# Adjacency layers with residual norms: where the second pair's norm steps and adjacency masks stand

## The chip, the cores and the metric

The kernel runs on one NeuronCore of a Trainium2 chip. The time is device microseconds of one execution; before the change the median of nine is 1879.75 us. TensorE multiplies matrices, VectorE, ScalarE and GpSimd do elementwise work and sums, SyncE issues the transfers. In the profile they are PE (its weight loads PEld), DVE, ACT, POOL and SP.

## The reference

There are 64 graphs of 256 nodes with 512 features, all float32. Two layers follow one another, each with a residual and a layer norm:

```python
deg = sum(adj, -1)                               # layer 0
agg = einsum('bij,bjf->bif', adj, x) / max(deg, 1e-6)
x   = layernorm(x + relu(concat([x, agg]) @ W.T))
q, k = split(x @ Wqk); v = x @ Wv                # layer 1
agg = einsum('bij,bjd->bid', adj, k * mask)
w   = mask * einsum('bid,bid->bi', q, agg) / sqrt(512)
x   = layernorm(x + softmax(w, over nodes)[:, :, None] * v)
```

The kernel folds Wq and Wk into one weight product (agg of x1 with q then stands for the scores), and masks adj by columns in place of masking k.

## The kernel before, in words

**Pairs and stages.** Two graphs are handled together, so there are 32 pairs, in the loop over `j` (line 760). A turn of the loop does layer 0 of pair `j` and layer 1 of pair `j - 1`. The first two turns are written out by themselves, since the pipeline is still filling: in turn 1, the normed features of pair 0 (`x1`) are transposed by TensorE (`turn_here`, line 625; its matmuls have line 629), while later turns send them through a transfer.

**Products in seven parts.** Each matrix product is made with seven block products in place of eight (the names P1 to P7). They need sums and differences of blocks of both operands: of the features (`outer_sums`, `fourth_sums`, `inner_sums`, tiles `xT_s`, `xT_i`, `x1T_s`, `x1T_i`, on VectorE and GpSimd), of the adjacency (`adj_sums`, tile `sa`, on GpSimd) and of the weights (`weight_sums`, tiles `t_i`, `t`, `w`, once, on VectorE). P1, P2, P3 and P5 are split once more by `inner` (line 340) into steps `first_two`, `second`, `third`, `last_two`; between them ScalarE copies PSUM banks that the next step's matmuls read or add into. At the end of P1 and P5 VectorE adds a fifth product to both banks (line 373) and, for P1, ScalarE then copies them to `own` (line 663). `own` holds the layer's result, `y` the operand of the aggregation, `z` its second half. `gather` (line 405) multiplies by the adjacency; its steps a to g are called u1, g2, g5, u2, u3, g3, u4.

**Order of the work.** Each engine works off its instructions in the order in which the program emits them. The order of the matmuls is written out by hand in strings: `run("i k m", ...)` takes the next step of unit i, then of k, then of m. The norms, masks, softmax and weight sums are side work: chains of small steps in `queue` (line 137). After each matmul step `tick` (line 152) looks for a chain's next step and emits it if its engine's planned time (`free`, by a cost formula) is not more than `room` ahead of the matmul clock: 0.6 us for VectorE and ScalarE. A `room` of -9.0 for VectorE shuts the planner's door on VectorE: its side steps stay in the queue, and in one chain a ScalarE step behind a VectorE step waits too. `quiet` stops the planner altogether. `flush(name)` (line 161) emits all that is left of a chain at that spot.

**The places that the change touches.** Layer norm 0 of pair 0 is queued at the end of turn 0 (`norm0`, line 525, rank 1): for each graph, two times `scaled` and `residual`, then `mean`, two `square`, `factor` (Ln and Exp), `shifts`, two `scale`. The masks of adj are four ScalarE steps (`mask_adj`, line 319, rank 4). The rest of the weight sums for layer 1 (`w1`, rank 9) is queued as well. In turn 1 the program runs P1, P5 and P2 interleaved (line 786), and later, once layer 0 is nearly done, transposes graph 0 of pair 0 (line 858), flushes the masks, makes the adjacency sums and loads rows of adj for pair 2 (lines 859 to 861), runs one step of P4, transposes graph 1 and makes the inner sums of the transposed features on GpSimd (line 864).

Of the kernel before, what the change touches and what calls it, by code (L numbers as in the profile page):

```python
# [94 lines left out]
def resnorm_kernel(  # L95
# [38 lines left out]
    gp = InOrder(tc, nc.gpsimd, clock, lambda name, n: 0.0)  # L134
    room = {vec: 0.6, act: 0.6}
# [25 lines left out]
    def flush(*names):  # L161
        while True:
            c = next((c for c in chains if not names or c[1] in names), None)
            if not c:
                return
            step(c)

    def run(order, **units):
        for name in order.split():
            units[name].pop(0)()  # L170
# [139 lines left out]
    def adj_sums(j):  # L310
        a, s = adjs[j], pool.tile([P, 4, 2, P], F32, name="sa", bufs=2)
        a11, a21, a12, a22 = (a[:, :, t, h * P:(h + 1) * P] for t in range(2) for h in range(2))
        gp.tensor_add(s[:, 0], a21, a22)
        gp.tensor_sub(s[:, 1], s[:, 0], a11)
        gp.tensor_sub(s[:, 2], a11, a21)
        gp.tensor_sub(s[:, 3], a12, s[:, 1])
        return {"A11": a11, "A12": a12, "A22": a22, "S1": s[:, 0], "S2": s[:, 1], "S3": s[:, 2], "S4": s[:, 3]}
# [307 lines left out]
    def turn_here(X, x1, k, ps):  # L625

        for t in range(NT):
            for c in range(NF):
                tc.keep_in_program_order(nc.tensor.matmul(  # L629
                    ps[t][:, c * P:(c + 1) * P], x1[:, k, t, c * P:(c + 1) * P], ident, is_transpose=True,  # L630
                    start=(c == 0), stop=True, skip_group_check=True))
            act.copy(X.a[:, k, :, :, t].rearrange("p h e m -> p (h e) m"), ps[t].rearrange("p (c m) -> p c m", c=NF))
# [125 lines left out]
    early = []  # L758

    for j in range(NP):  # L760
        X = Xs.pop(j)
        if j == 2:
            steady.append(True)
        flush("finish")
        owns[j] = pool.tile([P, 2, NT, F], F32, name="own", bufs=3)
        if j > 0:
            load_adj(j)
            run_now(late_sums)
            late_sums.clear()
            sumsA[j] = adj_sums(j)  # L770

        u, y, o = pf, py, pu
        ys[j] = pool.tile([P, 2, NT, F], F32, name="y")
        a1, a2, a3, a4, a5, a6, a7 = layer0(j, o, u, y)
        i = inner("P1", X, W0, pw[0], u, a1)
        k = inner("P5", X, W0, pw[1], y, a5)
        m = inner("P2", X, W0, pw[0], o, a2)
        p, q = pairs(u, X, S2, W0["T2"], a6), pairs(u, X, S3, W0["T3"], a7)
        r, s = inner("P3", X, W0, pw[1], y, a3), pairs(u, X, A22, W0["T4"], a4)
        if j == 0:  # L780
            run("i k i k i k i k", i=i, k=k)
            flush("degrees")
            load_rows(1)
        elif j == 1:
            early.append(a1)
            run("k i k m k i k", i=early[0], k=k, m=m)
            fourth_sums(X, [1])
            run("m p p", m=m, p=p)
            fourth_sums(X, [0])
            run("p p m", m=m, p=p)  # L790
            load_x(1)
        else:
            run("i k", i=i, k=k)
            send_scores(j - 2)
            run("i l k", i=i, k=k, l=open1)
            flush("norm")
            fetch_scores(j - 2)
            places[0](range(16))
            run("i k i k", i=i, k=k)
        if j != 1:  # L800
            fourth_sums(X, [1])
        if j > 1:
            flush("mask")
            sumsM[j - 1] = adj_sums(j - 1)
            if j + 1 < NP:
                load_rows(j + 1)
            load_x(j)
        if j > 1:
            softmax(j - 2)
            shared[0] = 1.0  # L810
        if j != 1:
            run("m p p", m=m, p=p)
            fourth_sums(X, [0])
            run("m p p m", m=m, p=p)
        flush("w0a")
        run("q q q", q=q)
        flush("w0")
        run("r q r m", m=m, q=q, r=r)
        if j == 1:
            flush("norm")  # L820
        quiet[0] = j < 2
        room[vec] = -9.0 if j > 1 else 0.6
        run("r s r", r=r, s=s)
        if j > 0:
            Y = x1Ts.pop(j - 1)
        if j > 1:
            inner_sums(Y, gp, 0)
            queue(1, "sums", *outer_sums(Y, vec), (vec, lambda Y=Y: inner_sums(Y, gp, 1)))
        T_late = []
        T = sums_T(ys[j], T_late, 0 if j < 2 else 1)  # L830

        if j == 0:
            degrees(1)
        zs[j] = pool.tile([P, 2, NT, HF], F32, name="z")
        g = gather(sumsA.pop(j), T, zs[j], pw[1], y[1], y[0], owns[j], rdegs[j], T_late)

        def sums_next():
            if j == NP - 1:
                return
            inner_sums(Xs[j + 1], gp, 0)  # L840
            rest = outer_sums(Xs[j + 1], gp)
            run_now(rest[:1])
            inner_sums(Xs[j + 1], gp, 1)
            late_sums.extend(rest[1:])
        if j == 0:
            sums_next()
            held = [c for c in chains if c[1] == "w1"]
            chains[:] = [c for c in chains if c[1] != "w1"]
            early.append(inner("P1", Xs[1], W0, pw[0], u, lambda fifth: early[1](fifth)))
            run("s s a b s c d i e i g f", s=s, i=early[0], **g)  # L850
            quiet[0] = False
        else:
            u2, o2, y2 = o, pf, y
            b1, b2, b3, b4, b5, b6, b7, b8 = layer1(j - 1, ys[j][:, :, 0], o2, u2, y2)
            jj = inner("P1", Y, W1, pw[0], u2)
            k = inner("P2", Y, W1, y[0], o2, b2)
            if j == 1:
                turn_here(Y, owns[0], 0, pw)
                flush("mask")
                sumsM[0] = adj_sums(0)  # L860
                load_rows(2)
                run("s", s=s)
                turn_here(Y, owns[0], 1, pw)
                inner_sums(Y, gp, 0)
                sums_Y = (*outer_sums(Y, vec), (vec, lambda: inner_sums(Y, gp, 1)))
                run("s a b s d c", s=s, **g)
                quiet[0] = False
                flush("w1")
                run("e j g f", j=jj, **g)
                queue(1, "sums", *sums_Y)  # L870
                run("k j k j k j", j=jj, k=k)
                b1(None)
                run("k", k=k)
            else:
                run("s s j s a b", s=s, j=jj, k=k, **g)
                room[vec] = 0.6
                run("j", j=jj)
                if j < NP - 1:
                    degrees(j + 1)
                run("c d j k e j", s=s, j=jj, k=k, **g)  # L880
                quiet[0] = True
                run("k", k=k)
                quiet[0] = False
                b1(None)
                run("g f", **g)
        flush("softmax", "adds", "sums", "degrees")
        if j > 0:
            aggs[j - 1] = late.tile([P, 2 * N_SIDE], F32, name="agg").rearrange(
                "p (k t f) -> p k t f", k=2, t=NT)
            vs[j - 1] = [late.tile([P, NT, F], F32, name="v", bufs=2) for _ in range(2)]  # L890
            T = sums_T(owns[j - 1])
            g = gather(sumsM.pop(j - 1), T, aggs[j - 1], pw[0], o2[1], o2[0])
            h, q = pairs(u2, Y, S2, W1["T2"], b6), pairs(u2, Y, S3, W1["T3"], b7)
            n = inner("P5", Y, W1, pw[1], y2, b5)
            p, open1 = pairs(u2, Y, A22, W1["T4"], b4), inner("P3", Y, W1, pw[1], y2, b3)
            norm0(j)
            mask_adj(j)
            run("k h h" if j > 1 else "h h", k=k, h=h)
            if j == 1:
                degrees(2)  # L900
                flush("degrees")
            if j < NP - 1:
                load_xT(j + 1)
            run("n k h h" if j > 1 else "n h h", k=k, n=n, h=h)
            fourth_sums(Y)
            shared[0] = 1.25
            sums_next()
            run("a n b q d q n c q e q n p g f", n=n, q=q, p=p, **g)
            b8()
            run("p l p l p l", p=p, l=open1)  # L910
            py, pu = pu, py
        else:
            norm0(0)
            mask_adj(0)
            chains.extend(held)
# [113 lines left out]
```

## Time and profile before

| | us |
|---|---|
| median of nine executions | 1879.75 |
| lowest and highest | 1878.16, 1880.83 |
| the profiled execution | 1880.45 |
| its span in the profile | 1878.6 |
| TensorE busy in the span | 1858.0 (99%) |
| VectorE busy | 1511.8 (80%) |
| ScalarE busy | 1308.9 (70%) |
| GpSimd busy | 908.8 (48%) |

A steady turn of the loop takes some 57 us: the transposed-operand matmuls of one turn that begin at 95.51 in the trace come again at 152.56. The granted clock of TensorE is 1.00 in that stretch. Rows of a timeline give the start in us from the span's start, the length, the engine, the line (90 for all that the three elementwise engines do, since a helper records it; 175 for matmuls, 629 for transposes), the operation, and the tile written and read; in brackets stand the idle time ahead of it and what ended that. A matmul of float32 with 512 columns advances TensorE by 0.86 us, one with 256 columns by 0.43; the lengths in the rows overlap with the row behind.

### The profile page before, as it was taken

Reading aid. Unit: us, or ns where it says so; the run is one execution under the profiler, and the core shown is the slowest. Engines: PE = TensorE matmul, PEld = TensorE weight load, DVE = VectorE, ACT = ScalarE, POOL = GpSimd, SP = SyncE. Lnnn points to the kernel's source line nnn. Section 1 sums busy time; section 2 is a strip of 40 time slices with the busy share of each in tenths; the row PEclk is TensorE's granted clock in tenths of the full one; section 3 lists DMA queues with packets and bytes.
Section 4 is the critical chain, followed back from the end, with each engine's and each line's share of the span. In section 5 each row is a group of like instructions: output and inputs, shape, how many; then the busy total and the mean of one; then the engine's idle time right before and its main releaser. Section 6 shows DMA issues by size and latency. Waiting matters only on the chain.

```text
span 1878.6 us, 25017 instructions
## 1 busy us (share of the span) xinstructions
PE 1858.0 (99%) x7002; PEld 1312.9 (70%) x7002; DVE 1511.8 (80%) x3180; ACT 1308.9 (70%) x3274; POOL 908.8 (48%) x1255
## 2 busy tenths in 40 slices
PE   9999999999999999999999999999999999999997
PEld 5667767767777677677677677677776777776775
DVE  7787888777888778887778887788877788877887
ACT  3667776777776677767677766777676777767766
POOL 5455453555443555444554435554445544355532
PEclk9999999999999999999999999999999999999998
DMA  6133334343333333343433343333434233433321
GB/s 225 57 74 82 99 90 119 85 104 88 101 96 99 104 85 98 96 111 85 110 83 101 95 103 100 85 100 99 106 85 115 80 101 95 110 94 85 100 64 51
DMA packets 380714, 181.27 MB, mean 96 GB/s; under 512 B 263712, under 2 KB 345248, under 8 KB 380576
## 3 DMA queue, kind: packets, MB, share of 16 engines
q1 hardware_dynamic: 380576, 179.67, 35.5%
q8 instruction: 57, 0.93, 0.2%
q14 instruction: 81, 0.66, 0.1%
HBM read 114.10 MB, written 34.06 MB: 79 GB/s over the span
## 4 chain that ended last, share of the span: by engine, by line
PE 94%; POOL 2%; issue 2%; DVE 1%; ACT 1%; POOLq 0%; ACTq 0%; DVEq 0%
PE bank L175 94%; POOL xT_i L90 1%; POOL xT_s L90 1%; POOL sa L90 1%; ACT own L90 1%; DVE v L90 0%; DVE own L90 0%; DVE turn L90 0%; ACT bank L90 0%; ACT x1T L90 0%; DVE bank L90 0%; PE bank L629 0%; DVE st L90 0%; ACT adj L90 0%; PE bank L652 0%
## 5 line engine op out<-in xcount | busy, mean ns | idle before, releaser
L90 ACT COPY bank<-bank 128x256 f32<-128x256 f32 (+1 forms) x768 | 332.5, 435 | 235.0 <-PE bank L175 222.3
L90 DVE TENSOR_TENSOR y<-bank,y 128x512 f32<-128x512 f32 x256 | 170.4, 686 | 132.7 <-ACT y L90 132.1
L90 ACT ACTIVATE own<-own,shift,rstd 128x512 f32<-128x512 f32 x255 | 199.8, 808 | 0.9 <-DVE shift L90 0.9
L175 PE MATMUL bank<-tv,sa 128*128 128x256 f32 x768 | 192.5, 380 | 0.9 <-DVE tv L90 0.9
L90 POOL TENSOR_TENSOR x1T_s<-x1T,x1T_s 128x256 f32<-128x256 f32 x64 | 63.6, 1012 | 267.8 <-PE bank L175 267.8
L90 POOL TENSOR_TENSOR x1T_i<-x1T_s 128x128 f32<-128x128 f32 x128 | 101.1, 790 | 183.1 <-DVE x1T_s L90 183.1
L90 ACT ACTIVATE junk<-own,less 128x512 bf16<-128x512 f32 x254 | 183.7, 723 | 3.0 <-DVE less L90 2.0
L175 PEld LDWEIGHTS bank<-tv,sa 128*128 128x128 f32 x768 | 145.4, 190 | 49.6 <-issue 22.9
L90 ACT COPY y<-bank 128x512 f32<-128x512 f32 x192 | 108.8, 583 | 95.2 <-PE bank L175 93.7
L90 POOL TENSOR_TENSOR sa<-adj 128x256 f32<-128x256 f32 x128 | 93.7, 732 | 167.6 <-DMA adj<-adj_t 153.8
L175 PE MATMUL bank<-w,x1T_s 128*128 128x512 f32 (+1 forms) x384 | 168.3, 521 | 0.0
L90 POOL TENSOR_TENSOR x1T_i<-x1T 128x256 f32<-128x256 f32 x64 | 55.1, 861 | 224.3 <-DMA x1T<-turn 211.5
L175 PE MATMUL bank<-t,xT_s 128*128 128x512 f32 (+1 forms) x384 | 159.7, 525 | 3.9 <-POOL sa L90 2.3
L90 DVE TENSOR_TENSOR v<-bank,v 128x512 f32<-128x512 f32 x186 | 119.1, 681 | 49.1 <-PE bank L175 49.1
L175 PE MATMUL bank<-t,x1T_s 128*128 128x512 f32 (+1 forms) x384 | 158.2, 521 | 0.3 <-ACT y L90 0.3
L175 PE MATMUL bank<-w,xT_s 128*128 128x512 f32 (+1 forms) x384 | 153.1, 521 | 0.0
L175 PE MATMUL bank<-t_i,xT_i 128*128 128x256 f32 x512 | 152.7, 380 | 0.3 <-POOL sa L90 0.2
L175 PE MATMUL bank<-t_i,x1T_i 128*128 128x256 f32 x512 | 152.2, 379 | 0.1
L175 PEld LDWEIGHTS bank<-t_i,x1T_i 128*128 128x128 f32 x512 | 97.1, 190 | 67.1 <-issue 49.8
L90 ACT COPY own<-bank 128x512 f32<-128x512 f32 x128 | 71.8, 587 | 92.8 <-PE bank L175 49.3
L175 PEld LDWEIGHTS bank<-t_i,xT_i 128*128 128x128 f32 x512 | 94.5, 189 | 58.3 <-issue 45.5
L175 PE MATMUL bank<-t,x1T 128*128 128x512 f32 x256 | 130.6, 592 | 0.0
(159 smaller groups left out, 4564.3 us busy)
## 6 DMA issues: line engine op xcount, KB each, us to landing
x<-x SPq DMA_DIRECT2D x64, 512.0 KB, 5.6
xT<-x_t SPq DMA_DIRECT2D x62, 512.0 KB, 5.5
out<-own SPq DMA_DIRECT2D x62, 512.0 KB, 3.2
x1T<-turn SPq DMA_DIRECT2D x480, 64.0 KB, 2.3
adj<-adj_t SPq DMA_DIRECT2D x64, 256.0 KB, 3.8
turn<-adj SPq DMA_DIRECT2D x64, 256.0 KB, 3.0
row<-d SPq DMA_DIRECT2D x31, 256.0 KB, 4.7
wqk<-wqk_t SPq DMA_DIRECT2D x4, 512.0 KB, 5.8
```

The costliest lines, as they stand in the source:

```text
L90: return self.tc.keep_in_program_order(getattr(self.engine, name)(out, *args, **kwargs))
L175: tc.keep_in_program_order(nc.tensor.matmul(ps, a, b, start=start, stop=True, skip_group_check=True))
```

## The change

In the second turn (`j == 1`) two things are different. First, after P1's and P5's first steps `room` of VectorE is set to -9.0 for the next five steps, and back to 0.6 behind them. In these steps the planner emits no VectorE side work; what is emitted directly, such as the additions at the end of P1 and P5, is not affected. Second, the flush of the masks, the adjacency sums and the load of rows stand behind the transposes of both graphs and the inner sums of the transposed features, where they stood between the two transposes. The order in which GpSimd makes `sa` and `x1T_i` is swapped by it. Since the planner's decisions depend on what was emitted before, the order of other side steps on VectorE and ScalarE in that turn differs too.

```diff
         elif j == 1:
             early.append(a1)
-            run("k i k m k i k", i=early[0], k=k, m=m)
+            run("k i k", i=early[0], k=k)
+            room[vec] = -9.0
+            run("m k i k", i=early[0], k=k, m=m)
+            room[vec] = 0.6
             fourth_sums(X, [1])
             run("m p p", m=m, p=p)
...
             if j == 1:
                 turn_here(Y, owns[0], 0, pw)
+                run("s", s=s)
+                turn_here(Y, owns[0], 1, pw)
                 flush("mask")
+                inner_sums(Y, gp, 0)
                 sumsM[0] = adj_sums(0)
                 load_rows(2)
-                run("s", s=s)
-                turn_here(Y, owns[0], 1, pw)
-                inner_sums(Y, gp, 0)
                 sums_Y = (*outer_sums(Y, vec), (vec, lambda: inner_sums(Y, gp, 1)))
                 run("s a b s d c", s=s, **g)
                 quiet[0] = False
```

## The prediction

> **What bounds the kernel now.** I read the page first, then the chain that ended last, then the list of who TensorE waited for, and last the timeline around the one pair that the change touches.
>
> ```profile
> span 1878.6 us, 25017 instructions
> PE 1858.0 (99%) x7002; PEld 1312.9 (70%) x7002; DVE 1511.8 (80%) x3180; ACT 1308.9 (70%) x3274; POOL 908.8 (48%) x1255
> ...
> PE bank L175 <- ACT own L90: 1.5, 4, 0.8
> ...
> PE bank L175 <- ACT x1T L90: 0.8, 1, 0.8
> PE bank L175 <- ACT y L90: 0.3, 1, 0.3
> PE bank L175 <- ACT bank L90: 0.3, 1, 0.3
> ```
>
> TensorE is busy 99% of the span and holds 94% of the chain, so an edit elsewhere counts only by the idle time it makes or removes on TensorE. The last lines give such waits over the whole span (total us, times, longest). The second pair runs once, from about 52 to 113 us of the span; before it hands over, TensorE waits there 0.82 us at 59.13, 0.35 at 69.71, 0.78 at 76.78 and 0.35 at 91.11. Removing all four would give 2.3 us, 0.12%: no gain of over 0.2% is there to be had. New waits have no such ceiling. TensorE's rows (start, length, operation, in brackets the idle time ahead and its releaser):
>
> ```profile
> 57.71 0.59 PE L175 MATMUL bank<-t_i,xT_i 128*128 128x256 f32 x2
> 59.13 3.67 PE L175 MATMUL bank<-t,xT_s 128*128 128x512 f32 x8 [0.82 <-ACT own L90]
> ...
> 69.71 0.67 PE L175 MATMUL bank<-w,xT_i 128*128 128x256 f32 x2 [0.35 <-ACT bank L90]
> 70.22 0.59 PE L175 MATMUL bank<-w,xT_s 128*128 128x256 f32 x2
> 70.65 1.02 PE L175 MATMUL bank<-t,agg 128*128 128x512 f32 x2
> 71.51 0.59 PE L175 MATMUL bank<-t_i,xT_s 128*128 128x256 f32 x2
> ...
> 76.78 1.99 PE L175 MATMUL bank<-y,adj 128*128 128x256 f32 x8 [0.78 <-ACT x1T L90]
> ```
>
> The same stretch on ScalarE and VectorE:
>
> ```profile
> 69.50 0.81 ACT L90 ACTIVATE own<-own,shift,rstd 128x512 f32<-128x512 f32 x1
> 70.42 0.57 ACT L90 COPY bank<-bank 128x512 f32<-128x512 f32 x1
> ...
> 73.97 1.31 ACT L90 ACTIVATE adj<-adj,mask_sb 128x256 f32<-128x256 f32 x3
> 75.18 0.58 ACT L90 COPY own<-bank 128x512 f32<-128x512 f32 x1
> 75.64 1.09 ACT L90 COPY x1T<-bank 128x512 f32<-128x512 f32 x2
> ...
> 57.93 1.42 DVE L90 TENSOR_TENSOR bank<-bank,fifth 128x256 f32<-128x256 f32 x4
> ...
> 60.56 0.68 DVE L90 TENSOR_TENSOR t<-t 128x256 f32<-128x256 f32 x1
> ...
> 66.71 0.42 DVE L90 TENSOR_TENSOR t_i<-w 128x256 f32<-128x256 f32 x1
> ...
> 83.22 0.69 DVE L90 TENSOR_TENSOR z<-bank,z 128x512 f32<-128x512 f32 x1
> ```
>
> **The change part by part.** No instruction is added or removed and TensorE's order is the same. What differs is the order on VectorE and ScalarE between 55 and 86 us and one swap on GpSimd; I compared the built orders of both kernels and priced the new order with the rows above, instruction by instruction.
>
> *Step 1, P1's additions first: a gain of about 1.0.* Before, VectorE ran four more norm steps of pair 0 (55.67 to 57.93), so the additions of the fifth product came at 57.93 though the products that they wait for (56.41 + 0.59) ended at 57.00; then ScalarE copied own from 58.40, and the matmul of 59.13 waited for it. Now the additions start at about 57.05, the first ends at 57.41, the copy runs 57.50 to 58.08, and the matmul starts at 58.23 (0.15 from the copy's end, as before: 58.40 + 0.58 to 59.13). That is 0.90 earlier. Up to 69.71 TensorE stays about 0.95 ahead: at that place ScalarE has the second square of the second batch element (0.72 a step) ahead of the bank copy, which I work out to 68.20 to 68.57, so the matmul comes at 68.72, 0.99 earlier, still with a wait of some 0.5.
>
> *Step 2, the norm steps arrive later: a new wait of 2.4.* The held steps of the second element (mean, two squares, Ln and Exp, the shift, two scalings) do not vanish. In the new order VectorE's shift stands behind the two 1024-wide weight sums, one y addition and the three additions to own (P2's end); and ScalarE has both scalings, which need that shift, ahead of the bank copy that P3's last matmuls read. That copy stood behind the scalings before too, but they were done by 70.31. VectorE: y addition 65.06 to 65.66 (starts: rows advance 0.60 to 0.64), weight sums 1.14 each to 67.94, y addition to 68.55, own additions 1.28 to 69.87, the one with the fifth to 70.48, shift done at 70.63. ScalarE: scalings from 70.70, 0.71 each to 72.12, bank copy 0.57 to 72.69. TensorE is through with the matmul ahead at 70.44 (68.72 + 0.43 + 0.43 + 0.86) and goes on at 72.84 instead of 71.51. So the lead of 0.99 turns into a lag of 1.33 (1.0 to 1.7 if each of the four hand-offs is 0.1 off). Queued behind that copy on ScalarE are the other copies of this stage, which wait for TensorE anyway.
>
> *Step 3, masks of adj: a gain of about 0.9.* Because VectorE is closed, the planner itself issues the three masks early on ScalarE (three of 0.40 at about 61.1 to 62.8, in slots where it waited for matmuls), so the flush behind the copies finds none left. The 1.31 of masks no longer stands between the transposes and the x1T copies. TensorE reaches the gather at 72.84 + 4.32 = 77.16, and the last x1T copy ends at 77.18 (own copy from 75.64, the x1T copies from 76.10, 0.51 apart, 0.57 long): start 77.23 against 76.78. The wait of 0.78 is gone; lag 0.45.
>
> *Step 4, VectorE's backlog of weight differences: a new wait of about 2.2.* Eight differences of w1 (P2's and P3's inner sums, 128x256) of which six were made at 66.71 to 70.0 now stand behind the last sum tv and ahead of the addition to z, which before started at 83.22. The matmul of 84.21 adds into the bank that this addition reads. New: tv's last sum starts at 81.69, the differences at 82.82 (before, 82.37). At the undisturbed pace (66.71 to 68.18: 1.47 for four) eight take 2.94, z runs 85.76 to 86.44, TensorE at 86.5. Beside GpSimd, whose eight sums now run 77.2 to about 84 (its rows: 2.9 and 3.7 a group of four), one of these took up to 0.68. If all eight took 0.68 (5.44), TensorE would go on at 89.0. I take 0.4 more than undisturbed, since GpSimd's work covers only the first two or three: 86.9, against 84.21 before: lag 2.7. Ends: 2.3 and 4.8.
>
> *Step 5, what moves at no cost.* GpSimd makes x1T's inner sums ahead of adj's: the first come earlier than they did relative to TensorE, and the adj sums are read from 98.52 on, over 10 us after they are made. x's load waits for the last residual addition of pair 0 on SP's queue (58.05 before, about 62 now), and the rows of adj and the next xT queue behind it; they take 3.0 to 5.6 us, and their first readers are at 94.02 (the degrees) and 100.06 on GpSimd, so 25 us are spare. If that cover were gone, 4 us would be lost. Past 87 us VectorE has slack of 1.85 at 90.0 and TensorE is full, so the lag stays to the end.
>
> The sum is -0.99 + 2.32 - 0.88 + 2.25 = 2.7 us. The profiled run took 1880.45 (span 1878.6, 1.85 around it), 0.70 above the median of 1879.75; its own time would become 1883.15, the median 1882.45. That is 0.14%.
>
> The granted clock is 1.00 in every stretch of this trace that I read, over waits of at most 0.9 us in them; a wait of 2.4 is not in it. [...]
>
> **The rivals.**
> - *VectorE's backlog decides (slower).* Over 0.2%, here 3.76 us and about what a measurement of this kernel can tell from no change, is reached when the eight differences of step 4 take 4.0 us, 0.50 each, rather than 3.34. For it: the 0.68 beside GpSimd, and tv rows of 1.12 and 1.21 against 0.68. Against it: GpSimd is done by about 84. At 0.55 each: +4.1, 1883.9; at the end of the rows +4.8.
> - *The clock or a further wait adds to the lags.* The longest wait of TensorE rises from 0.9 to 2.4; a disturbance that costs as much again as half of it is +3.9, 1883.7. Nothing in the trace shows one.
> - *The new waits do not come (gain).* If step 2's copy were ready when TensorE needs it and the backlog fitted the slots, only the removals remain: 0.99 + 0.78 = 1.8, 1878.0. Against it: the built order has both scalings ahead of that copy and all eight differences ahead of z.
> - *The change does nothing.* The masks' move alone would be the 0.78; but the order on both engines does change, so no.
>
> **How the numbers follow.** Forecast 0.63 (+1.6 to +3.6); backlog +4.1 0.16; clock or further wait +3.9 0.10; gain 0.09; nothing 0.02. Slower by over 0.2%: 0.26. Faster by over 0.2% would need more than every wait of the pair: 0.02. Within: 0.72. The range reaches from step 4's wait all but missing (2.7 - 2.1 = +0.6) to the end of the backlog case (+5.0): 1880.4 to 1884.8.
>
> **What would show it.** Right: matmul bank<-t,xT_s near 58.2; the first own scalings of the second element near 70.7 and a TensorE wait of about 2.4 <-ACT bank at 72.8; no wait <-ACT x1T of 0.78; eight t_i/w rows on VectorE at 83 to 86 and a wait of about 2.2 <-DVE z near 86.9. Wrong: a granted clock under 1.00 there, a first wait that stays at 59.1, or a lag that is worked off after 95 us.

## The result and the profile after

The changed kernel takes 1884.23 us (median of ten, 1882.06 to 1885.86) where the kernel before, with the runs made beside it, takes 1878.90 (median of thirty). The ratio is 1.0028, with a 95% interval of 1.0020 to 1.0036: the change costs 0.28%, between 3.8 and 6.8 us. The profiled execution of the changed kernel took 1883.76, with a span of 1882.0.

TensorE's waits over the whole span, the first two of the list, longest total first (total us, times, longest):

```profile
PE bank L175 <- ACT bank L90: 2.3, 2, 2.0
PE bank L175 <- DVE z L90: 2.2, 1, 2.2
```

The wait of 2.2 for z is new, and so is that of 2.0 in the first line (the other 0.3 of it was there before). Before, no wait of the second pair was over 0.82, and the longest in the whole span was 1.2, at the start. The wait of 0.78 for x1T and that of 0.82 for own are gone. TensorE's rows of the second pair in the changed kernel (start, length, operation, idle time ahead and its releaser):

```profile
57.98 3.67 PE L175 MATMUL bank<-t,xT_s 128*128 128x512 f32 x8
...
68.56 0.67 PE L175 MATMUL bank<-w,xT_i 128*128 128x256 f32 x2 [0.35 <-ACT bank L90]
...
72.52 0.79 PE L175 MATMUL bank<-t_i,xT_s 128*128 128x256 f32 x2 [2.00 <-ACT bank L90]
73.09 1.06 PE L175 MATMUL bank<-w,xT_i 128*128 128x256 f32 x2
73.95 1.91 PE L629 MATMUL bank<-ident,own 128*128 128x128 f32 x8
...
78.71 1.99 PE L175 MATMUL bank<-y,adj 128*128 128x256 f32 x8
...
88.87 1.13 PE L175 MATMUL bank<-y,sa 128*128 128x256 f32 x4 [2.19 <-DVE z L90]
89.84 0.83 PE L175 MATMUL bank<-t_i,x1T_i 128*128 128x256 f32 x2
90.45 1.06 PE L175 MATMUL bank<-w,x1T 128*128 128x256 f32 x2
91.31 1.92 PE L175 MATMUL bank<-t_i,x1T_i 128*128 128x256 f32 x4
```

The rows directly behind the two waits are to be looked at. Eight transposes of 1.04 us before (72.37) take 1.91 here, and four matmuls of t_i that took 1.35 before (85.93) take 1.92. The same engine does the same work more slowly. The table of stretches says why (columns: stretch, its length, then busy time of PE, PEld, DVE, ACT, POOL with instructions, then the granted clock, DMA share and GB/s):

```profile
70.50:72.50 2.00, 0.02 (x1) 0.00 (x0) 0.00 (x0) 2.00 (x4) 0.00 (x0) 1.00 0.24 75
72.50:75.90 3.40, 3.38 (x13) 3.01 (x14) 1.60 (x3) 0.85 (x3) 0.00 (x0) 0.57 0.00 0
75.90:79.30 3.40, 3.40 (x15) 1.84 (x15) 1.07 (x2) 2.15 (x4) 0.98 (x2) 0.92 0.00 0
79.30:86.70 7.40, 7.17 (x29) 4.83 (x27) 6.72 (x12) 2.11 (x4) 5.96 (x7) 1.00 0.00 0
86.70:88.90 2.20, 0.03 (x1) 0.03 (x1) 2.17 (x7) 0.00 (x0) 0.00 (x0) 1.00 0.00 0
88.90:92.30 3.40, 3.40 (x11) 2.64 (x12) 2.93 (x6) 0.36 (x1) 0.89 (x1) 0.67 0.00 0
92.30:95.70 3.40, 3.40 (x15) 2.68 (x14) 0.61 (x1) 2.44 (x6) 1.67 (x4) 0.83 0.00 0
```

In the first and fifth stretch TensorE stands still; in the two stretches behind each, the granted clock is 0.57 and 0.92, and 0.67 and 0.83. Lost at that clock are 3.4 x (0.43 + 0.08) = 1.7 and 3.4 x (0.33 + 0.17) = 1.7 us. In the profile of before the granted clock is 1.00 all the way from 4.7 to 1868 us.

The two engines that make the waits, in the changed kernel:

```profile
69.67 0.69 DVE L90 TENSOR_TENSOR own<-own,fifth 128x512 f32<-128x512 f32 x1
70.28 0.15 DVE L90 TENSOR_TENSOR shift<-less,rstd 128x2 f32<-128x2 f32 x1
...
83.55 1.21 DVE L90 TENSOR_TENSOR tv<-y,tv 128x512 f32<-128x512 f32 x1
84.68 0.94 DVE L90 TENSOR_TENSOR t_i<-w 128x256 f32<-128x256 f32 x1
...
87.80 0.42 DVE L90 TENSOR_TENSOR t_i<-w,t_i 128x256 f32<-128x256 f32 x1
88.13 0.68 DVE L90 TENSOR_TENSOR z<-bank,z 128x512 f32<-128x512 f32 x1
...
70.47 1.52 ACT L90 ACTIVATE own<-own,shift,rstd 128x512 f32<-128x512 f32 x2 [1.60 <-DVE shift L90]
71.89 0.57 ACT L90 COPY bank<-bank 128x512 f32<-128x512 f32 x1
```

ScalarE stands 1.60 us for the shift, which VectorE makes only behind the last addition to own; then come two scalings, and behind them the bank copy that TensorE waits for. Later VectorE goes through all eight weight differences (84.68 to 88.1) before the addition to z.

**Where the time went, in one account.** The changed execution is 0.33 us ahead before the change begins (its matmul of the pair's first step starts at 51.33, that of before at 51.66), so 0.33 is added to each difference. Lag behind before: -0.82 at the matmul of 57.98 (59.13 before), -0.82 at 68.56 (69.71), +1.34 at 72.52 (71.51), +2.26 at 78.71 (76.78), +4.99 at 88.87 (84.21), +6.45 at the adjacency matmul of 101.63 (95.51). From there to the end the two spans come 2.7 us closer, step by step at short waits of the later pairs: the execution of before has ten there for sa and three for own with 3.0 us in all, that of after six and one with 1.6, and each costs somewhat more than its length. These waits differ from profile to profile (three to eleven for sa in the kernels below), and the medians, 5.3 us apart, are the better measure.

### The profile page after: what moved, and what is told of

Same layout as the page of the kernel before. It is cut to its first block, busy times and chain, and to the rows that moved or that the text cites. A ratio compares the mean times of both kernels' runs of the same rounds, so it can differ in the third digit from the quotient of the medians.

```text
span 1882.0 us, 25016 instructions
## 1 busy us (share of the span) xinstructions
PE 1860.0 (99%) x7002; PEld 1315.5 (70%) x7002; DVE 1509.2 (80%) x3180; ACT 1309.5 (70%) x3274; POOL 910.7 (48%) x1255
## 4 chain that ended last, share of the span: by engine, by line
PE 94%; POOL 2%; DVE 2%; issue 1%; ACT 1%; POOLq 0%; DVEq 0%; ACTq 0%
PE bank L175 94%; POOL xT_i L90 1%; POOL xT_s L90 1%; POOL sa L90 0%; ACT own L90 0%; DVE own L90 0%; PE bank L629 0%; DVE v L90 0%; DVE tv L90 0%; DVE t_i L90 0%; ACT bank L90 0%; DVE turn L90 0%; DVE w L90 0%; DVE bank L90 0%; DVE st L90 0%
```

## The experiments

Two theories, A and B, stand against each other on what makes the loss, and a third, C, is on the clock: A (the held norm and weight steps make two waits, and each wait lowers the clock) and B (the second part of the change does, by the swap on GpSimd and the later loads), C (the low clock is not a consequence of the waits).

**One part alone: VectorE's closed door.**

```diff
-            run("k i k m k i k", i=early[0], k=k, m=m)
+            run("k i k", i=early[0], k=k)
+            room[vec] = -9.0
+            run("m k i k", i=early[0], k=k, m=m)
+            room[vec] = 0.6
```

> Only the first part of the change: VectorE takes no norm steps ahead of P1's last additions; masks, adjacency sums and the load of rows stay where they were. VectorE and ScalarE then run in the same order as in the whole change, since the planner issues the masks early by itself. Theory A (the loss of the whole change is two new waits of TensorE, each followed by some 1.5 to 1.9 us at a lower granted clock, both made by the norm and weight steps that were held back): still slower than before by 4.5 to 6 us, with both waits there; the second may be up to 0.4 shorter, since GpSimd makes the adjacency sums earlier. Theory B (the swap on GpSimd and the later transfers make the loss): within 1 us of before or faster by 0.8.

Measured: 1885.13 against 1878.97, ratio 1.0031 (1.0019 to 1.0043). This part alone is 6.2 slower, a little more than the 4.5 to 6 expected, and so makes all of the loss; B falls. The waits are not the same, though. TensorE's in the second pair of this kernel, and rows of VectorE and GpSimd:

```profile
PE bank L175 <- ACT bank L90: 3.8, 2, 2.9
PE bank L175 <- DVE z L90: 0.8, 1, 0.8
...
65.00 0.94 DVE L90 TENSOR_TENSOR t<-t 128x256 f32<-128x256 f32 x1
65.87 0.95 DVE L90 TENSOR_TENSOR t_i<-t,t_i 128x256 f32<-128x256 f32 x1
...
64.76 0.91 POOL L90 TENSOR_TENSOR sa<-adj 128x256 f32<-128x256 f32 x1
65.62 0.90 POOL L90 TENSOR_TENSOR sa<-adj,sa 128x256 f32<-128x256 f32 x1
```

The masks are early here too, so GpSimd makes the adjacency sums at 63 to 66.5, beside the weight differences on VectorE: these take 0.94 where they take 0.42 in the whole change. The shift comes at 72.12 in place of 70.28 (with the start 0.30 later, 1.5 of it is this), and the first wait grows to 2.9. In exchange GpSimd is free at 84.3, all eight later differences run at 0.42, and the wait for z is 0.78. Of the second part's two effects, the one is a gain and the other a loss of about the same size, which I had put at 0.4 and on one side only. Behind the wait of 0.78 the clock stays at 1.00; around and behind that of 2.9 it is 0.71 in 72 to 76 and 0.50 in 76 to 80.

**The other part alone: masks behind the copies.**

```diff
                 turn_here(Y, owns[0], 0, pw)
-                flush("mask")
-                sumsM[0] = adj_sums(0)
-                load_rows(2)
                 run("s", s=s)
                 turn_here(Y, owns[0], 1, pw)
+                flush("mask")
                 inner_sums(Y, gp, 0)
+                sumsM[0] = adj_sums(0)
+                load_rows(2)
```

> Only the second part: masks, adjacency sums and the load of rows behind the transposes. VectorE's and TensorE's orders are those of before; on ScalarE the three masks stand behind the x1T copies. Theory A: the wait of 0.78 for x1T goes, no new one comes, 0.8 us faster than before (too little to tell by time, plain in the trace). Theory B: slower than before by 2 us or more.

Measured: 1878.68 against 1878.97, ratio 0.9998 (0.9989 to 1.0007). The gather starts at 75.92 in place of 76.78, so the wait for x1T is gone, 0.86 gained. At 83.83 (84.21 before) 0.38 of it is left and at 95.23 (95.51) 0.28: a wait of 0.19 for tv is new, and GpSimd, whose sums now come later, runs beside VectorE's tv sums and a weight difference (0.94). A gain of 0.3 us, too little for the time to tell.

**The first wait alone taken away.** The norm's steps up to the shift stay where they were; its two scalings go behind P3's bank copies on ScalarE.

```diff
         if j == 1:
-            flush("norm")
+            for c in [c for c in chains if c[1] == "norm"]:
+                while len(c[3]) > NT:
+                    step(c)
...
         run("r s r", r=r, s=s)
+        if j == 1:
+            flush("norm")
```

> The whole change, but the two last scalings of the held norm stand behind the two bank copies of P3's third step on ScalarE; VectorE's order is that of the change. Theory A: the wait of 2.0 at 72.5 goes and with it the stretch of lower clock behind it (the gather starts near 74.8 in place of 78.7), the wait of 2.2 for z and the second low stretch stay: 3.9 us faster than the change, 1.4 to 2.5 slower than before. Theory C (the lower clock is not a consequence of the waits, or costs nothing): 2.0 faster than the change, about 3.3 slower than before, and the clock still under 1.00 in 72 to 80.

Measured: 1880.17 against 1878.97, ratio 1.0009 (1.0001 to 1.0018): 1.2 slower than before where 1.4 to 2.5 were expected, so some 4 us of the change's 5.3 are given back by moving two instructions of 0.8 behind two of 0.6 and 0.4. The gather starts at 75.91 in an execution that is 0.81 behind at the start of the pair, so at 75.10 when counted from before's start; the changed kernel's is at 79.04 by that count, 3.9 later. That is more than the wait of 2.0, as A says and C does not. But A's second half did not come out in this profile:

```profile
86.07 1.13 PE L175 MATMUL bank<-y,sa 128*128 128x256 f32 x4 [2.20 <-DVE z L90]
...
83.80:86.07 2.27, 0.07 (x2) 0.00 (x1) 2.24 (x7) 0.00 (x0) 0.00 (x0) 1.00 0.00 0
86.07:89.50 3.43, 3.37 (x14) 2.58 (x15) 2.96 (x6) 0.92 (x3) 0.89 (x1) 1.00 0.00 0
89.50:93.00 3.50, 3.23 (x15) 2.49 (x14) 1.38 (x3) 2.43 (x7) 1.68 (x4) 1.00 0.00 0
```

The wait of 2.20 is there, and the clock stays at 1.00. The eleven executions of this kernel lie in two groups, seven from 1879.09 to 1880.25 and four from 1881.60 to 1881.96, with the middle ones 2.0 apart; the profiled one is of the lower group. The mean granted clock of an execution, over its whole span, is 0.997 in all four of the upper group and 0.998 in six of the seven of the lower. The same wait thus seems to lower the clock in some executions and not in others.

**The second wait alone taken away.** All eight weight differences go behind both additions to z; the planner's clock for VectorE is kept as it was, so that nothing later moves.

```diff
-                flush("w1")
+                rest = next(c for c in chains if c[1] == "w1")
+                chains.remove(rest)
+                vec.free = max(vec.free, clock[0]) + len(rest[3]) * (0.07 + HF / 960)
                 run("e j g f", j=jj, **g)
+                planned = vec.free
+                run_now(rest[3])
+                vec.free = planned
```

> The whole change, but the eight weight differences that stood ahead of the addition to z stand behind both additions to z; ScalarE's order is that of the change. Theory A: the wait of 2.2 for z goes and with it the lower clock at 90 to 95: 3.7 us faster than the change, 1.6 to 2.8 slower than before; the wait of 2.0 at 72.5 and its low stretch stay. Theory C: 2.2 faster than the change, 3.1 slower than before.

Measured: 1882.98 against 1878.97, ratio 1.0021 (1.0012 to 1.0030), 4.0 slower than before where I had expected 1.6 to 2.8. The wait for z is gone, the clock stays at 1.00 behind 80 us, but there is a wait that I had missed (waits of the second pair):

```profile
PE bank L175 <- ACT bank L90: 2.3, 2, 2.0
PE bank L175 <- DVE t_i L90: 1.1, 1, 1.1
```

P2's first matmul of layer 1 reads the first two of those differences and comes right behind the addition to z. The wait of 2.0 stayed, with the clock at 0.69 in 72 to 76.

**Both waits taken away.** The edit of the third experiment, and of the eight differences the first two stay ahead of z.

```diff
-                flush("w1")
+                rest = next(c for c in chains if c[1] == "w1")
+                chains.remove(rest)
+                vec.free = max(vec.free, clock[0]) + len(rest[3]) * (0.07 + HF / 960)
+                planned = vec.free
+                run_now([rest[3].popleft() for _ in range(2)])
+                vec.free = planned
                 run("e j g f", j=jj, **g)
+                planned = vec.free
+                run_now(rest[3])
+                vec.free = planned
```

> The whole change with both new waits taken away: the two last scalings stand behind P3's bank copies on ScalarE, and of the eight weight differences only the two that P2's first matmul needs stay ahead of the addition to z, the other six go behind both additions. Theory A: no wait over 0.4 between 52 and 95 us, the granted clock 1.00 throughout, and of the step gains what the profile of the change showed stays: 0.8 at P1's copy and 0.8 at the x1T copies, less what later waits take back; the adjacency matmuls at the head of the stage come 1.0 to 1.8 earlier than before, measured from the same start, 0.05% to 0.1% faster and so hardly to be told by time. Theory C (the loss lies elsewhere in the change): still 2 us or more slower than before.

Measured: 1878.03 against 1878.51, ratio 0.9996 (0.9987 to 1.0006). All of the loss is gone. TensorE's longest waits in the second pair:

```profile
PE bank L175 <- ACT y L90: 0.5, 1, 0.5
PE bank L175 <- ACT bank L90: 0.3, 1, 0.3
```

The clock is 1.00 in every stretch from 52 to 115 us. The adjacency matmul starts at 94.84 (95.51 before, with this execution 0.10 behind at the start), so 0.8 is gained, a little under the 1.0 to 1.8 expected: a wait of 0.54 for y stands where one of 0.35 was, and a wait of 0.18 for tv remains. It is no version that the time can tell from before.

**What a wait costs by itself.** The kernel before, with dummy subtractions on VectorE ahead of an addition to z in 28 steady turns; a second kernel with fewer of them.

```diff
...
             act.copy(r22, of(u))
+            for _ in range(delay[0] if own is not None else 0):
+                tc.keep_in_program_order(nc.vector.tensor_sub(idle, idle, idle))
             vec.tensor_add(r22, of(p5), r22)
...
+        delay[0] = 8 + (j - 3) % 7 if 2 < j < NP - 1 else 0
```

> The kernel before, with dummy subtractions on VectorE (128x256, about 0.34 each) ahead of the first addition of the aggregation's u3 step in 28 steady turns, 8 to 14 of them, so that TensorE gets one wait of about 1.3 to 3.4 us in each turn, four of every length. It leaves no part of the computation out. [...] Theory A2 (a length decides): there is one length from which every wait lowers the clock and below which none does.

> The kernel before with the same dummy subtractions, but 4 to 7 of them in a turn: by the last run's step of 0.45 us for each more of them, waits of TensorE of about 0.4, 0.85, 1.3 and 1.75 us, seven of each. In the run with 8 to 14, waits of 2.2 to 2.8 lowered the granted clock in 7 of 8 turns, at 1.7 to 1.8 us each. [...] Theory A2 (one length near 2.0 to 2.2 decides): none in all 28 turns.

The first kernel took 2046.48 us and the second 1917.28, one execution each. The waits came out longer in the first than I had meant, 2.2 to 5.1. For every wait I took its length from TensorE's row, the granted clock of the 9 us behind it, and the time from its end to the adjacency matmul, 6.99 where the clock stays at 1.00:

| wait, us | turns | with a lower clock | time lost behind it |
|---|---|---|---|
| 0.36 to 0.53 | 7 | 0 | 0 |
| 0.82 to 0.83 | 7 | 0 | 0 |
| 1.28 to 1.40 | 7 | 0 | 0 |
| 1.74 to 1.86 | 7 | 0 | 0 |
| 2.20 to 2.77 | 8 | 7 | 1.6 to 1.7 |
| 3.12 to 3.71 | 8 | 7 | 1.4 to 3.0 |
| 4.04 to 5.08 | 12 | 12 | 2.4 to 3.0 |

C falls: waits put in by hand, with nothing else changed in TensorE's order, lower the clock. A2 falls too: of three waits of 2.20 and 2.21 in the first kernel two lowered it and one didn't, and a wait of 3.71 didn't. A wait of 2.20, one of 2.21 and that of 3.71 in the first kernel, each with the stretches behind it (columns as above):

```profile
202.90:206.20 3.30, 1.10 (x6) 0.62 (x5) 3.13 (x8) 1.33 (x5) 0.05 (x1) 1.00 0.00 0
206.20:209.60 3.40, 3.40 (x12) 2.37 (x13) 3.33 (x9) 3.10 (x6) 0.00 (x0) 1.00 0.00 0
209.60:213.00 3.40, 3.40 (x13) 2.28 (x12) 3.37 (x8) 2.88 (x9) 0.00 (x0) 1.00 0.63 184
...
1087.80:1091.10 3.30, 1.11 (x6) 0.62 (x4) 3.13 (x8) 1.37 (x5) 0.07 (x1) 1.00 0.02 5
1091.10:1094.50 3.40, 3.39 (x9) 2.56 (x10) 3.33 (x9) 3.07 (x6) 0.00 (x0) 0.64 0.00 0
1094.50:1097.90 3.40, 3.40 (x12) 2.08 (x11) 2.49 (x6) 1.26 (x4) 0.00 (x0) 0.86 0.66 177
...
1717.20:1722.00 4.80, 1.09 (x7) 0.61 (x5) 4.52 (x11) 1.35 (x5) 0.17 (x1) 1.00 0.00 0
1722.00:1725.40 3.40, 3.40 (x12) 2.38 (x13) 3.33 (x9) 3.09 (x6) 0.00 (x0) 1.00 0.00 0
1725.40:1728.80 3.40, 3.40 (x13) 2.28 (x12) 3.37 (x8) 2.89 (x9) 0.00 (x0) 1.00 0.69 189
```

Behind the second wait the clock is 0.64 and 0.86, behind the first and the third 1.00. So the length alone does not decide; what else does is left open. What a longer wait costs is also in the clock: over the 9 us behind a wait it is 0.81 to 0.84 where 1.4 to 1.7 us were lost, and 0.66 to 0.73 where 2.4 to 3.0 were.

By the two groups of times in the third experiment, with their middle ones 2.0 apart, one kernel seems to lose some 1.7 us at a wait in one execution and nothing in the next. The spread of the changed kernel fits this too: an estimate from the account above is 3.0 slower with neither wait hit (6.45 less twice 1.7) and 6.4 with both, against 1878.90 that is 1881.9 to 1885.3, and its executions took 1882.06 to 1885.86, with a mean granted clock of 0.998 and 0.997 in the two shortest (1882.06 and 1882.13) and 0.996 in the three longest (1885.43 to 1885.86). It was not seen in two profiles of one kernel.

## Why the prediction was right or wrong, point by point

- **The bound.** Right that no gain of over 0.2% was to be had. "Counts only by the idle time it makes or removes on TensorE" was too narrow: at the low clock TensorE lost some 3.4 us while it was busy.
- **Step 1, P1's additions first.** Right: 0.82 gained at the first matmul, 0.90 predicted; 0.82 at the second wait, where 0.99 was predicted.
- **Step 2, the norm steps arrive late.** Right in place and releaser, and near in size: a wait of 2.00 <-ACT bank where 2.4 was predicted, in part since TensorE came to it with a smaller lead (0.82, not 0.99); +1.34 of lag at that matmul against +1.33 predicted, and the shift at 70.28 and the scalings at 70.47, both within 0.35 of the working. The third experiment shows that the two scalings ahead of the bank copy are the cause.
- **Step 3, the masks.** The wait for x1T went, as worked out. The lag there was 2.26 and not 0.45: some 1.7 of the 1.8 between them is the low clock of 73.0 to 76.4, not the masks.
- **Step 4, the weight differences.** Right in place and near in size: a wait of 2.19, the lag grows by 2.73 where 2.25 was predicted. Of the 0.48 between, about 0.4 had come by 84.71 (lag 2.64), with a wait of 0.18 for tv among it, ahead of the differences. Those took 3.45 (84.68 to 88.13) where 3.34 was predicted. The cover by GpSimd reached the first difference alone (0.94).
- **Step 5, what costs nothing.** Right: x's load was issued at 61.91, and no wait of TensorE up to 115 us goes back to a transfer.
- **The clock. Here the prediction failed**: its sum has nothing for a lower clock, which it left as a rival with a chance of 0.10; a granted clock under 1.00 was its own sign of being wrong. The row that it set out from was sound (1.00 over waits of at most 0.9 us), but it did not bear on waits of 2.0. The runs put a price on it: 1.7 us for the low clock behind each of the two waits of the changed kernel, and 1.6 to 1.7 behind seven of the eight waits of 2.2 to 2.8 put in by hand.
- **The number.** Without the low clock the account gives 6.45 less twice 1.7, 3.0 us, where the sum said 2.7; with it, 5.3 by the medians. So the term that failed is the clock's, put at nothing, and the waits were sized about right. That the median of 1884.23 lies in the range (1880.4 to 1884.8) is luck in two ways. The range's upper end was set by the backlog of VectorE, which did not come. And the range was counted from 1879.75, while the runs of before made beside the change have 1878.90: as a lag, 5.3 is over the range's end of +5.0. The likeliest case, 1882.45 and within 0.2%, was wrong: the change is slower by 0.28%. What happened is the second rival, the clock added to the lags: it was priced at +3.9, and with both waits hit it is more. The first rival, VectorE's backlog, and the gain did not come. The first rival's price was also off by the prediction's own sum: eight differences at 0.50 each give 2.7 + 0.66 = 3.4, so the 3.76 are reached at 0.55 each, and +4.1 at about 0.59.

## What to carry to other kernels

Where TensorE is busy 99% of the time, a wait of it of 2 us or more must be priced at its own length and, by these runs, some 1.7 us more (up to 3.0 for waits over 3), since the granted clock was low behind both waits of the changed kernel (2.00 and 2.19) and behind 26 of the 28 waits of 2.20 to 5.08 put in by hand; waits up to 1.86 cost their length alone in these runs. Whether two shorter ones close together add up, no run shows. Closing an engine to side work does not remove that work: look up where each held instruction ends in every engine's order, and which copy or addition, on which TensorE waits, then stands behind it. When a queue is reordered, ask of each instruction put back who reads it first: the eight weight differences could not all go behind z, but six could.

## What the runs showed of the hardware that was not expected

- Of the waits put in by hand none of 28 up to 1.86 us lowered the granted clock, 7 of 8 from 2.20 to 2.77 did, and 19 of 20 above. One fall costs 1.6 to 1.7 us for waits up to 2.8, 1.4 to 3.0 for waits of 3.1 to 3.7, and 2.4 to 3.0 for waits over 4.
- The same wait at the same place need not lower the clock: in the third experiment's profile it did not (2.20 us, clock 1.00), in the changed kernel's it did (2.19 us, clock 0.67).
- Float32 differences of 128x256 on VectorE took 0.42 alone and 0.94 beside GpSimd's sums of float32, and those sums 0.90 against 0.72: which engine's sums run at the same time moved a wait of TensorE by 0.9 us.
